# Summing squares over embeddings: on VectorE inside a tile, or by accumulating DMAs

## The chip, the cores and the metric

The kernel runs on one core of one Trainium2 chip. A core has TensorE (PE, matrix products), VectorE (DVE), ScalarE (ACT), GpSimd (POOL) and SyncE (SP), which run side by side, each through its own instructions in order, and wait for one another at semaphores. Sixteen DMA engines move data between DRAM, the on-chip memory SBUF and themselves; a DMA is issued by SP, ACT or POOL, and whoever needs its result waits for its semaphore. PE writes its products into PSUM, which has eight banks of 128 x 512 fp32 numbers.

The metric is the device time of one execution in microseconds, lower is better.

## What is computed

The reference, cut to what matters (batch b = 1024, features f = 512, outputs m = 512, embeddings e = 64, all fp32):

```
out_lin = x @ lin_w.T + lin_b
xv = einsum('bf,efm->bem', x, weight)
zp = einsum('bf,efm->bem', square(x), square(weight))
y = out_lin + 0.5 * sum(square(xv) - zp, axis=1)
```

The large part is `xv`: 64 products of 1024 x 512 by 512 x 512, whose squares are summed over the 64 embeddings. The second sum needs no product per embedding: the squares of weight are summed over e first (`w2_sum`), and one product with the squares of x closes the kernel.

## The kernel before, in words

**Groups.** The 64 embeddings' weights are seen as one matrix of 512 rows and 64 x 512 columns. A group takes 2048 of its columns, and there are 16 groups. Within a group the product of x (1024 x 512) with the group's block (512 x 2048) is done by two nested levels of a seven-product scheme (Strassen's, in Winograd's form): the outer level cuts the weights into four quadrants `w11`, `w12`, `w21`, `w22`, each in two halves `.0` and `.1` of 128 x 1024 numbers (128 partitions, two rows of 512 columns), 512 KB each. A group is thus eight loads of 512 KB (`load`, L378).

**Outer level.** `outer_sum` (L384) forms on VectorE the combinations T1 = w12 - w11, T2 = w22 - T1, then overwrites w12 with w22 - w12 and w21 with w21 - T2. The seven outer products, in the order 1, 6, 2, 7, 4, 5, 3 (`ORDER`), are seven calls of `tree` (L416) with the right operands w11, T2, w21, w12, w21 (overwritten by then), T1, w22.

**Inner level.** `tree` forms four combinations `t1` to `t4` of 128 x 512 on POOL (L427), issues seven pairs of matmuls into PSUM (L438), and lets ACT copy banks out (L287) and VectorE and POOL add the products up in `oa`, `ob`, `c`, `p` (sums with both operands in SBUF may go to either engine, L274; those that read PSUM go to VectorE). The trees for i = 2, 3, 4 and 5 end four result tiles each, one per `pos`: that is 16 tiles of 128 x 1024 per group, all entries of `xv` for this block.

**Sum over embeddings.** On the host the weights are laid out so that a block of 512 columns holds 8 outputs with their 64 embeddings side by side. So the sum over embeddings is a sum over 64 neighbouring columns of a tile. `finish` (L402) squares a result tile on ACT in place and has VectorE reduce it (L296) from 128 x 1024 to 128 x 16 numbers in `acc`, which SP stores to DRAM once per group (`acc_dram`, 128 KB). `w_squares` (L394) does the same for the eight weight halves: ACT squares a half into one of two buffers `wsq` and VectorE reduces it into `w2_sum`.

**Order of the work.** The instructions of each engine are put in order by a planner in the kernel (`Plan`, L27): each operation has a cost per engine it may run on, what it reads and writes, and, for a DMA, a time `land` until its data is there. The sequence of the matmuls is fixed by keys. Latest start times are worked out backward from it, and a list scheduler then takes, on each engine, the most urgent ready operation. Operations with a choice between VectorE and POOL go where the planner finds room. The order so found is then emitted, and each engine follows it strictly.

**Start and end.** Before the first group, x, `lin_w` and the bias are loaded and the linear part is computed and parked in DRAM (`lin_dram`). After the last group, x is loaded again and squared, `acc_dram` and `lin_dram` are read back, half-adds `lin + 0.5 * acc` run on VectorE (L546), the closing products of the squares of x with `w2_sum` follow on PE (L565), and the results are stored.

Of the kernel before, what the change touches and what calls it, by code (L numbers as in the profile page):

```python
# [23 lines left out]
PE, DVE, ACT, POOL, SP = "PE", "DVE", "ACT", "POOL", "SP"  # L24


class Plan:  # L27

    HOP = 0.18
# [138 lines left out]
def kernel(  # L175
# [7 lines left out]
):  # L183

    nc = tc.nc
    NG, NQ, _, NCB, KH, N = weight.shape
    B = xT.shape[1]
    M = out.shape[1]
    NB = B // P
    NK = 2 * KH
    MG = M // NG
    MI = MG // 4  # L210
    E = N // MI
    H = B // 2
    Q = B // 4

# [1 line left out]
    dram = ctx.enter_context(  # L216
        tc.tile_pool(name="dram", bufs=1, space=bass.MemoryType.DRAM)
    )
# [6 lines left out]
    buf = {}  # L225

    def make(name, shape, pool=sb):
        buf[name] = pool.tile(shape, F32, tag=name, name=name)
        return name

    def ring(tag, n, shape, pool=sb):
        names = [make(f"{tag}_{i}", shape, pool) for i in range(n)]
        state = [0]

        def take():
            state[0] += 1
            return names[(state[0] - 1) % n]

        return take
# [13 lines left out]
    make("b1", [P, G, N], ps)  # L253
    make("b3", [P, G, N], ps)
    b2_ring = ring("b2", 2, [P, G, N], ps)
    acc_ring = ring("acc", 2, [P, NB, MG])
    w2_sum = sb.tile([P, NK, M], F32, tag="w2_sum", name="w2_sum")
    bias = sb.tile([P, M], F32, tag="bias", name="bias_sb")
    acc_dram = dram.tile([P, NB, M], F32, tag="accd", name="accd")
    lin_dram = dram.tile([P, NB, M], F32, tag="lind", name="lind")  # L260

    plan = Plan()
# [21 lines left out]
    def act(o, i, func, reads, writes, cost=1.04):  # L284
        def emit(_):
            if func is None:
                nc.scalar.copy(o, i)  # L287
            else:
                nc.scalar.activation(o, i, func)  # L289

        plan.add({ACT: cost}, emit, reads, writes)

    def reduce(o, i, reads, writes):
        plan.add(
            {DVE: 1.14},
            lambda _: nc.vector.tensor_reduce(  # L296
                o, i.rearrange("p a (m e) -> p a m e", e=E), axis=AX.X, op=ALU.add
            ),
            reads, writes,
        )  # L300

    def dma(o, i, reads, writes, cost=2.4, land=1.5, queue=nc.sync):
        plan.add({SP: cost}, lambda _: queue.dma_start(o, i), reads, writes, land=land)
# [14 lines left out]
    for k in range(NK):  # L318
        q, r = divmod(k, KH)
# [15 lines left out]
    for g, bank in enumerate(lin_banks):  # L335
        o = ("ob2", "ob3", "c_0", "c_1")[g]
# [23 lines left out]
    for i in ORDER:  # L360
        x = buf[f"X{i}"]
# [11 lines left out]
    QUAD = ("w11", "w12", "w21", "w22")  # L373

    def w(g, q):
        return q + "ab"[g % 2] if q == "w22" else q

    def load(g):  # L378
        for q in (0, 1, 3, 2):
            for c in range(NCB):  # L380
                n = f"{w(g, QUAD[q])}.{c}"
                dma(buf[n], weight[g, q][:, c], (), (n,))

    def outer_sum(g, which):  # L384
        o, a, b = {
            1: ("T1", "w12", "w11"),
            2: ("T2", w(g, "w22"), "T1"),
            3: ("w12", w(g, "w22"), "w12"),
            4: ("w21", "w21", "T2"),
        }[which]  # L390
        for c in range(NCB):
            whole(f"{o}.{c}", f"{a}.{c}", f"{b}.{c}", True, DVE)

    def w_squares(g, q):  # L394
        row, col = divmod(QUAD.index(q), 2)
        for c in range(NCB):
            n, sq = f"{w(g, q)}.{c}", wsq_ring()
            act(buf[sq], buf[n], AF.Square, (n,), (sq,), 1.07)
            m = g * MG + (2 * col + c) * MI
            reduce(w2_sum[:, ts(row, KH), m:m + MI], buf[sq], (sq,), (("w2", row, m),))  # L400

    def finish(g, i, n, pos):  # L402

        row, col = {2: (0, 0), 3: (0, 1), 4: (1, 0), 5: (1, 1)}[i]
        q, cc = divmod(pos, 2)
        b, m = (row * 2 + q) * G, (col * 2 + cc) * MI
        act(buf[n], buf[n], AF.Square, (n,), (n,), 1.07)
        reduce(buf[acc_name[g]][:, b:b + G, m:m + MI], buf[n], (n,), ((acc_name[g], i, pos),))
# [4 lines left out]
    acc_name = {}  # L413
    acc_parts = [(i, pos) for i in (2, 3, 4, 5) for pos in range(4)]

    def tree(s, g, i):  # L416
        r = [f"{w(g, RHS[i])}.{c}" for c in range(NCB)]
# [33 lines left out]
        def outer_psum(b, pos):  # L451

            if i == 1:
                copy(f"oa{pos}", b)
            elif i == 5:
                for n in (f"oa{pos}", f"ob{pos}"):
                    whole(n, n, b, psum=True)
                finish(g, i, f"oa{pos}", pos)
            else:
                o = target(pos)  # L460
                whole(o, b, f"{ADDEND[i]}{pos}", psum=True)
                if i in (2, 4, 3):
                    finish(g, i, o, pos)

        def outer_sbuf(b, p, pos):

            if i == 1:
                whole(f"oa{pos}", b, p, psum=True)
            elif i == 5:
                whole(p, b, p, psum=True)  # L470
                for n in (f"oa{pos}", f"ob{pos}"):
                    whole(n, n, p)
                finish(g, i, f"oa{pos}", pos)
            else:
# [21 lines left out]
        outer_psum(b2, 2)  # L496

    for g in range(NG):
        acc_name[g] = acc_ring()
        load(g)  # L500
        outer_sum(g, 1)
        outer_sum(g, 2)
        w_squares(g, "w12")
        for idx, i in enumerate(ORDER):
            if i == 1:
                w_squares(g, "w11")
            if i == 2:
                w_squares(g, "w21")
            if i == 7:
                outer_sum(g, 3)  # L510
            if i == 4:
# [10 lines left out]
    last = acc_name[NG - 1]  # L522
    edge = M - MG
    acc_all = ("T2.0", "T2.1", w(NG, "w22") + ".0", w(NG, "w22") + ".1")
    lin_all = ("w21.0", "w21.1", "T1.0", "T1.1")
    for (h, q), n in xe.items():
        dma(buf[n], x_src[:, ts(q, KH), ts(h, H)], (), (n,))
    for g in range(NB // G):
        n, a = lin_all[g], acc_all[g]
        dma(buf[a][:, :, 0:edge], acc_dram[:, ts(g, G), 0:edge],  # L530
            tuple(("accd", x) for x in range(NG - 1)), (a,))
        dma(buf[n], lin_dram[:, ts(g, G), :], (), (n,))
# [9 lines left out]
    def add_acc(g, lo, hi, a, reads):  # L542
        l = buf[lin_all[g]][:, :, lo:hi]
# [8 lines left out]
    for g in range(NB // G):  # L552
        rows = {0: (2, 3), 1: (4, 5)}[g // 2]
        reads = tuple((last, i, 2 * (g % 2) + c) for i in rows for c in range(2))
        add_acc(g, edge, M, buf[last][:, ts(g, G), :], reads)

    out_dst = out.rearrange("(n p) m -> p n m", p=P)
    w2_parts = tuple(("w2", row, m * MI) for row in range(2) for m in range(M // MI))
    for g, bank in enumerate(("b3", "b1", "b2_0", "b2_1")):
        o = acc_all[g]  # L560
        h = g // 2
# [52 lines left out]
```

## Time and profile before

| | |
|---|---|
| device time, median of 2 runs | 1438.42 us (1438.36 to 1438.48) |
| profiled execution, span from first to last instruction | 1436.8 us (its own device time is not given beside the span) |
| PE busy | 1408.8 us, 98% |
| VectorE busy | 1245.7 us, 87% |
| POOL busy | 1149.6 us, 80% |
| ACT busy | 748.8 us, 52% |
| DMA, main queue (SP's): share of the 16 engines | 18.1% |
| moved in all | 83.54 MB |

How to read it. Busy time is the time in which an engine carried out instructions; issuing a DMA and waiting do not count. A group row of the profile gives source line, engine, operation, output <- inputs, shapes and count; then busy time in us and the mean of one in ns; then the idle time before these instructions and whom they waited for. A row of the waits reads "who waited <- for whom: us in total, times, longest". A row of a window gives its bounds, its length, the busy time of PE, PEld (the loading of weights into PE), DVE, ACT and POOL, PE's granted clock (1.00 is full), the share of the DMA engines and GB/s. A row of the chain of waits or of the order of time begins with start and duration in us. A row of the DMA issues ends with size and the time from issue to landing.

### The profile page before, as it was taken

The numbers are of one execution on the slowest core, as the hardware profiler recorded it, in microseconds if no ns is written. First come the engines' busy times: TensorE is split into PE (matmuls) and PEld (weight loads), VectorE is DVE, ScalarE is ACT, GpSimd is POOL, SyncE is SP. The second block draws the span as 40 slices with busy tenths as digits, with TensorE's granted clock in tenths as the row PEclk, the third lists the DMA queues.
The fourth block names the chain that finished last, engine by engine and source line by source line (L and its number), as shares of the span: only waits on it lengthen the run. The fifth ranks groups of instructions, "written<-read, shape, count | busy, mean of one in ns | idle before, by whom it ended". The sixth has DMA issues, their size and how long they took to land.

```text
span 1436.8 us, 10763 instructions
## 1 busy us (share of the span) xinstructions
PE 1408.8 (98%) x3264; PEld 619.3 (43%) x3264; DVE 1245.7 (87%) x1006; ACT 748.8 (52%) x756; POOL 1149.6 (80%) x691
## 2 busy tenths in 40 slices
PE   7999999999999999999999999999999999999998
PEld 3444444444444444444444444444444444444443
DVE  1899898998989899898988989899898888989984
ACT  1465554645545465564556555465554546556441
POOL 6988886878878688896878888687887868889781
PEclk9999999999999999999999999999999999999999
DMA  5311111111111112111111111111111111210221
GB/s 212 117 60 58 48 59 33 59 48 59 59 42 51 33 59 62 46 58 33 59 48 58 59 48 59 33 59 48 58 59 45 53 32 57 60 52 22 88 74 59
DMA packets 40377, 83.54 MB, mean 58 GB/s; under 512 B 18240, under 2 KB 19264, under 8 KB 40320
## 3 DMA queue, kind: packets, MB, share of 16 engines
q1 hardware_dynamic: 39664, 81.54, 18.1%
q10 hardware_dynamic: 576, 1.05, 0.2%
q8 instruction: 27, 0.44, 0.1%
q14 instruction: 30, 0.25, 0.1%
q0 software_dynamic: 80, 0.26, 0.0%
HBM read 76.68 MB, written 6.16 MB: 58 GB/s over the span
## 4 chain that ended last, share of the span: by engine, by line
PE 90%; POOL 4%; DVE 2%; issue 1%; ACT 1%; DMA 1%; DVEq 0%; POOLq 0%; SPq 0%
PE b L438 86%; POOL oa L274 3%; PE b L325 2%; PE b L565 2%; ACT p L287 1%; POOL t L274 1%; DMA ob<-lin_wT 0%; DVE p L274 0%; DMA T1.1_83<-lind 0%; DVE ob L274 0%; DVE w11.1_73 L536 0%; DVE w21.0_76 L274 0%; DVE oa L274 0%; DVE acc L296 0%; DVE w11.0_72 L536 0%
## 5 line engine op out<-in xcount | busy, mean ns | idle before, releaser
L438 PE MATMUL b<-t,X 128*128 128x512 f32 x1792 | 806.2, 592 | 2.0 <-DVE p L274 1.6
L438 PEld LDWEIGHTS b<-t,X 128*128 128x128 f32 x1792 | 340.0, 190 | 431.9 <-issue 415.0
L287 ACT COPY p<-b 128x1024 f32<-128x1024 f32 x224 | 225.6, 1007 | 266.1 <-PE b L438 226.8
L289 ACT ACTIVATE oa<-oa 128x1024 f32<-128x1024 f32 x128 | 131.9, 1054 | 165.3 <-DVE oa L274 90.9
L296 DVE TENSOR_REDUCE w_sum<-wsq 128x16 f32<-128x1024 f32 x128 | 154.8, 1211 | 29.0 <-ACT wsq L289 28.9
L287 ACT COPY b<-b 128x1024 f32<-128x1024 f32 x112 | 111.8, 998 | 91.1 <-PE b L438 85.2
L274 DVE TENSOR_TENSOR p<-b,p 128x1024 f32<-128x1024 f32 x96 | 117.0, 1218 | 43.4 <-PE b L438 43.4
L296 DVE TENSOR_REDUCE acc<-oa 128x16 f32<-128x1024 f32 x128 | 152.0, 1207 | 0.0
L438 PE MATMUL b<-w21.0_76,X 128*128 128x512 f32 x256 | 120.3, 592 | 0.0
L274 POOL TENSOR_TENSOR oa<-oa,p 128x1024 f32<-128x1024 f32 x32 | 102.8, 3212 | 1.8
L289 ACT ACTIVATE c<-c 128x1024 f32<-128x1024 f32 x64 | 67.7, 1058 | 67.8 <-DVE c L274 67.8
L274 POOL TENSOR_TENSOR oa<-p,oa 128x1024 f32<-128x1024 f32 x32 | 75.7, 2365 | 27.2 <-DVE p L274 26.9
L274 DVE TENSOR_TENSOR oa<-b,p 128x1024 f32<-128x1024 f32 x64 | 78.0, 1219 | 11.7 <-PE b L438 10.8
L274 POOL TENSOR_TENSOR c<-c,oa 128x1024 f32<-128x1024 f32 x32 | 75.4, 2357 | 13.8 <-DVE c L274 11.7
L274 POOL TENSOR_TENSOR oa<-oa,ob 128x1024 f32<-128x1024 f32 x32 | 76.4, 2387 | 6.9 <-DVE oa L274 6.9
L274 POOL TENSOR_TENSOR ob<-ob,oa 128x1024 f32<-128x1024 f32 x32 | 76.3, 2384 | 5.5 <-DVE ob L274 5.5
L274 POOL TENSOR_TENSOR t<-w21.0_76,t 128x512 f32<-128x512 f32 x32 | 40.8, 1275 | 48.3 <-PE b L438 48.3
L274 POOL TENSOR_TENSOR ob<-p,ob 128x1024 f32<-128x1024 f32 x32 | 75.7, 2364 | 0.5 <-DVE p L274 0.5
L296 DVE TENSOR_REDUCE acc<-ob 128x16 f32<-128x1024 f32 x64 | 75.9, 1209 | 0.0
L296 DVE TENSOR_REDUCE acc<-c 128x16 f32<-128x1024 f32 x64 | 74.8, 1208 | 1.1 <-ACT c L289 1.1
L438 PEld LDWEIGHTS b<-w21.0_76,X 128*128 128x128 f32 x256 | 48.6, 190 | 61.2 <-issue 61.2
L274 DVE TENSOR_TENSOR ob<-b,oa 128x1024 f32<-128x1024 f32 x32 | 39.1, 1223 | 40.5 <-PE b L438 39.8
(127 smaller groups left out, 2295.9 us busy)
## 6 DMA issues: line engine op xcount, KB each, us to landing
w11.0_72<-weight SPq DMA_DIRECT2D x16, 512.0 KB, 3.7
w11.1_73<-weight SPq DMA_DIRECT2D x16, 512.0 KB, 3.8
w12.0_74<-weight SPq DMA_DIRECT2D x16, 512.0 KB, 3.8
w12.1_75<-weight SPq DMA_DIRECT2D x16, 512.0 KB, 3.8
w21.0_76<-weight SPq DMA_DIRECT2D x16, 512.0 KB, 3.8
w21.1_77<-weight SPq DMA_DIRECT2D x16, 512.0 KB, 4.7
w22a.0_78<-weight SPq DMA_DIRECT2D x8, 512.0 KB, 3.8
w22a.1_79<-weight SPq DMA_DIRECT2D x8, 512.0 KB, 3.8
```

Source lines behind the costliest of these rows:

```text
L274: f(o, a, b)
L287: nc.scalar.copy(o, i)
L289: nc.scalar.activation(o, i, func)
L296: lambda _: nc.vector.tensor_reduce(o, i.rearrange("p a (m e) -> p a m e", e=E), axis=AX.X, op=ALU.add),
L325: nc.tensor.matmul(buf[bank][:, j, :], buf[f"oa{2 * h + q}"][:, r, ts((g * G + j) % (NB // 2), P)], buf[f"ob{q}"][:, r, :], start=(k == 0) ...
L438: nc.tensor.matmul(buf[b][:, j, :], buf[f"X{i}"][:, SLOT[p], ts(j, P)], op, start=first, stop=True, skip_group_check=True,)
L565: nc.tensor.matmul(buf[bank][:, j, :], buf[xe[h, k // KH]][:, k % KH, ts((g * G + j) % (NB // 2), P)], w2_sum[:, k, :], start=(k == 0), st ...
```

## The change

The host lays the weights out so that a block of 512 columns is one embedding with all its 512 outputs; a group is four embeddings, one pair of quadrant and half each. The sum over embeddings then is a sum of whole tiles. It is no longer done on VectorE: each squared tile is added to a running sum by a DMA that POOL issues with `accum_op=ALU.add` (the first tile of each sum by a plain copy from SP's queue). The squares of weight are added into `w2_sum` in SBUF, in two places (one per row of quadrants). The squares of the results are added into two DRAM sums `acc_dram[0]` and `acc_dram[1]`, in four places each. DMAs into the same place are put one after another by a dependence on the place (`key`). The eight last result tiles (trees 5 and 3 of the last group) are not stored but added on VectorE at the end (`tail`), and at the end both DRAM sums are read back whole.

```diff
-    MG = M // NG
-    MI = MG // 4
-    E = N // MI
...
-    acc_ring = ring("acc", 2, [P, NB, MG])
...
-    acc_dram = dram.tile([P, NB, M], F32, tag="accd", name="accd")
+    NS = 2
+    acc_dram = [
+        dram.tile([P, NB, M], F32, tag=f"accd{s}", name=f"accd{s}") for s in range(NS)
+    ]
...
-    def reduce(o, i, reads, writes):
-        plan.add(
-            {DVE: 1.14},
-            lambda _: nc.vector.tensor_reduce(
-                o, i.rearrange("p a (m e) -> p a m e", e=E), axis=AX.X, op=ALU.add
-            ),
-            reads, writes,
-        )
+    started = set()
+
+    def accumulate(o, i, reads, key):
+
+        if key in started:
+            plan.add(
+                {POOL: 0.9},
+                lambda _: nc.gpsimd.dma_start(o, i, accum_op=ALU.add),
+                reads, (key,), land=5.0,
+            )
+        else:
+            started.add(key)
+            dma(o, i, reads, (key,))
...
     def w_squares(g, q):
-        row, col = divmod(QUAD.index(q), 2)
+        row = QUAD.index(q) // 2
         for c in range(NCB):
             n, sq = f"{w(g, q)}.{c}", wsq_ring()
             act(buf[sq], buf[n], AF.Square, (n,), (sq,), 1.07)
-            m = g * MG + (2 * col + c) * MI
-            reduce(w2_sum[:, ts(row, KH), m:m + MI], buf[sq], (sq,), (("w2", row, m),))
+            accumulate(w2_sum[:, ts(row, KH), :], buf[sq], (sq,), ("w2", row))
+
+    tail = []
 
     def finish(g, i, n, pos):
 
-        row, col = {2: (0, 0), 3: (0, 1), 4: (1, 0), 5: (1, 1)}[i]
+        row = {2: 0, 3: 0, 4: 1, 5: 1}[i]
         q, cc = divmod(pos, 2)
-        b, m = (row * 2 + q) * G, (col * 2 + cc) * MI
+        pair = row * 2 + q
         act(buf[n], buf[n], AF.Square, (n,), (n,), 1.07)
-        reduce(buf[acc_name[g]][:, b:b + G, m:m + MI], buf[n], (n,), ((acc_name[g], i, pos),))
+        if g == NG - 1 and i in (5, 3):
+            tail.append((pair, n))
+        else:
+            accumulate(acc_dram[cc % NS][:, ts(pair, G), :], buf[n], (n,), ("acc", pair, cc % NS))
...
-        if g + 1 < NG:
-            names = tuple((acc_name[g], *k) for k in acc_parts)
-            dma(acc_dram[:, :, ts(g, MG)], buf[acc_name[g]], names, names + (("accd", g),))
...
+    def add_half(g, n):
+        l = buf[lin_all[g]]
         plan.add(
-            {DVE: 0.15 + 1.09 * (hi - lo) / N},
-            lambda _: nc.vector.scalar_tensor_tensor(l, a, 0.5, l, ALU.mult, ALU.add),
-            reads + (lin_all[g],), (lin_all[g],),
+            {DVE: 1.24},
+            lambda _: nc.vector.scalar_tensor_tensor(l, buf[n], 0.5, l, ALU.mult, ALU.add),
+            (n, lin_all[g]), (lin_all[g],),
         )
 
     for g in range(NB // G):
-        add_acc(g, 0, edge, buf[acc_all[g]][:, :, 0:edge], (acc_all[g],))
...
+        for s in range(NS):
+            dma(buf[acc_all[g]], acc_dram[s][:, ts(g, G), :], (("acc", g, s),), (acc_all[g],))
+            add_half(g, acc_all[g])
+    for pair, n in tail:
+        add_half(pair, n)
...
-    w = w.reshape(n_e, p, 2, n_k // 2, groups, 2, 2, m_in).transpose(4, 2, 5, 1, 6, 3, 7, 0)
+    w = w.reshape(groups, 2, 2, p, 2, n_k // 2, width).transpose(0, 4, 1, 3, 2, 5, 6)
```

Counted over the whole program: 384 reductions (256 of results, 128 of weights) and 15 stores of `acc` go; 366 accumulating DMAs of 512 KB on POOL (240 into the DRAM sums, 126 into `w2_sum`), 10 plain copies of 512 KB on SP, and 8 more half-adds of 128 x 1024 come. The planner also gives 27 of the sums of 128 x 1024 that POOL had to VectorE. PE's matmuls, ACT's copies and squares and the weight loads stay the same in number and size.

More of the change, by code (lines that the diff above doesn't have):

```diff
@@ L412 @@
     RHS = {1: "w11", 2: "w21", 3: "w22", 4: "w21", 5: "T1", 6: "T2", 7: "w12"}
-    acc_name = {}
-    acc_parts = [(i, pos) for i in (2, 3, 4, 5) for pos in range(4)]
     def tree(s, g, i):
@@ L515 @@
             tree(7 * g + idx, g, i)
-        if g + 1 < NG:
-            names = tuple((acc_name[g], *k) for k in acc_parts)
-            dma(acc_dram[:, :, ts(g, MG)], buf[acc_name[g]], names, names + (("accd", g),))
     xe = {(h, q): (f"w11.{q}", f"w12.{q}")[h] for h in range(2) for q in range(2)}
-    last = acc_name[NG - 1]
-    edge = M - MG
     acc_all = ("T2.0", "T2.1", w(NG, "w22") + ".0", w(NG, "w22") + ".1")
@@ L528 @@
     for g in range(NB // G):
[L529 to L532, printed above, removed]
+        dma(buf[lin_all[g]], lin_dram[:, ts(g, G), :], (), (lin_all[g],))
     for n in xe.values():
@@ L540 @@
         )
-    def add_acc(g, lo, hi, a, reads):
-        l = buf[lin_all[g]][:, :, lo:hi]
+    def add_half(g, n):
+        l = buf[lin_all[g]]
         plan.add(
-            {DVE: 0.15 + 1.09 * (hi - lo) / N},
-            lambda _: nc.vector.scalar_tensor_tensor(l, a, 0.5, l, ALU.mult, ALU.add),
-            reads + (lin_all[g],), (lin_all[g],),
+            {DVE: 1.24},
+            lambda _: nc.vector.scalar_tensor_tensor(l, buf[n], 0.5, l, ALU.mult, ALU.add),
+            (n, lin_all[g]), (lin_all[g],),
         )
     for g in range(NB // G):
-        add_acc(g, 0, edge, buf[acc_all[g]][:, :, 0:edge], (acc_all[g],))
[L552 to L555, printed above, removed]
+        for s in range(NS):
[3 more added lines that the diff above has]
+        add_half(pair, n)
     out_dst = out.rearrange("(n p) m -> p n m", p=P)
-    w2_parts = tuple(("w2", row, m * MI) for row in range(2) for m in range(M // MI))
+    w2_parts = (("w2", 0), ("w2", 1))
     for g, bank in enumerate(("b3", "b1", "b2_0", "b2_1")):
@@ L591 @@
     n_e, n_f, n_m = w.shape
-    p, n_k, width = 128, n_f // 128, 512
-    m_in = width // n_e
-    groups = n_m // (4 * m_in)
-    w = w.reshape(n_e, p, 2, n_k // 2, groups, 2, 2, m_in).transpose(4, 2, 5, 1, 6, 3, 7, 0)
+    p, n_k, width = 128, n_f // 128, n_m
+    groups = n_e // 4
+    w = w.reshape(groups, 2, 2, p, 2, n_k // 2, width).transpose(0, 4, 1, 3, 2, 5, 6)
     arrays = {
```

1 line of the change is left out of this document (removed).

## The prediction

> **What bounds the kernel now.** I read the busy shares first, then the chain that ended last, then one steady stretch of it, and last the waits.
>
> ```profile
> span 1436.8 us, 10763 instructions
> PE 1408.8 (98%) x3264; PEld 619.3 (43%) x3264; DVE 1245.7 (87%) x1006; ACT 748.8 (52%) x756; POOL 1149.6 (80%) x691
> PE 90%; POOL 4%; DVE 2%; issue 1%; ACT 1%; DMA 1%; DVEq 0%; POOLq 0%; SPq 0%
> ...
> 293.37 79.25 PE b L438 x184
> 373.24 3.29 POOL oa L274
> 377.52 1.00 ACT p L287
> 378.57 79.25 PE b L438 x184
> ...
> 300.00:385.20 85.20, 84.39 (x198) 37.15 (x197) 76.26 (x62) 46.46 (x48) 69.43 (x42) 1.00 0.17 51
> ```
>
> The reader is to see a kernel that is TensorE from end to end. The chain repeats every 85.20 us (293.37 to 378.57), which is one of the 16 groups; in such a stretch PE is busy 84.39 us at a granted clock of 1.00, DVE 76.26, POOL 69.43. So DVE, whose reductions the change takes away, is not the bound. Nor can much be won: 2% less than the median of 1438.42 is 1409.7, and PE alone is busy 1408.8. The question is therefore whether PE keeps being fed. The sums are made against the profiled execution (span 1436.8); the median lies 1.6 above that span, which I take as what lies around it, so an amount that is added to the span is added to 1438.
>
> **What is removed.**
>
> ```profile
> L296 DVE TENSOR_REDUCE w_sum<-wsq 128x16 f32<-128x1024 f32 x128 | 154.8, 1211 | 29.0 <-ACT wsq L289 28.9
> L296 DVE TENSOR_REDUCE acc<-oa 128x16 f32<-128x1024 f32 x128 | 152.0, 1207 | 0.0
> L296 DVE TENSOR_REDUCE acc<-ob 128x16 f32<-128x1024 f32 x64 | 75.9, 1209 | 0.0
> L296 DVE TENSOR_REDUCE acc<-c 128x16 f32<-128x1024 f32 x64 | 74.8, 1208 | 1.1 <-ACT c L289 1.1
> accd<-acc SPq DMA_DIRECT2D x15, 128.0 KB, 2.4
> ```
>
> 384 reductions, 457.5 us of DVE, and 15 stores of 128 KB. DVE gets 27 sums of 128x1024 from POOL and 8 more half-adds at the end; at 1.2 to 2.3 us each (rows below) that is some 40 to 80 us, and DVE falls to about 850 of 1437. On the end of the kernel this gain is worth nothing, because PE did not wait for a reduction:
>
> ```profile
> PEld b L438 <- POOL t L274: 9.6, 31, 1.2
> PEld b L438 <- DVE w_sum L296: 1.2, 5, 0.2
> ACT wsq L289 <- DVE w_sum L296: 1.8, 4, 1.2
> ```
>
> The third row is the one to remember: a square buffer came free after a 1.2 us reduction, and ACT waited for one 1.8 us in the whole run.
>
> **What is added.** 384 squares of 128x1024 (512 KB each) are summed elsewhere: 8 by half-adds on DVE, 10 first ones by plain copies on SP's queue, and 366 (126 into w2_sum, 240 into the two DRAM sums) by accumulating DMAs issued by POOL. Per group that is 23. Each has three prices: POOL's time to issue, the DMA engines' time, and the time until it lands.
>
> ```profile
> 305.79 0.33 SPq L303 DMA_DIRECT2D w11.0_72<-weight  x1
> ...
> L308 POOL DMA_DIRECT2D bias_sb<-lin_b x1 | 0.7, 677 | 0.8 <-POOLq L603 0.8
> L274 POOL TENSOR_TENSOR ob<-ob,p 128x1024 f32<-128x1024 f32 x17 | 41.1, 2417 | 2.3 <-DVE p L274 2.3
> L274 DVE TENSOR_TENSOR oa<-b,p 128x1024 f32<-128x1024 f32 x64 | 78.0, 1219 | 11.7 <-PE b L438 10.8
> L274 DVE TENSOR_TENSOR ob<-ob,p 128x1024 f32<-128x1024 f32 x15 | 34.2, 2282 | 0.0
> L274 POOL TENSOR_TENSOR t<-w12.0_74,t 128x512 f32<-128x512 f32 x16 | 20.4, 1273 | 4.5 <-PE b L438 4.5
> POOL t L274 <- PE b L438: 118.8, 124, 3.2
> POOL t L274 <- DVE w12.0_74 L274: 47.0, 15, 3.1
> POOL oa L274 <- DVE p L274: 26.9, 15, 1.8
> POOL t L274 <- DVE w21.0_76 L274: 18.6, 16, 1.2
> ```
>
> *POOL's issue.* The only DMA that POOL issues before took it 677 ns. 366 x 0.677 = 247.8 us. Bounds: 0.33 us, what SP needs to issue a load in the order of time, and 1.27 us, a POOL sum of half size. I take 0.677, the only row of POOL's own. POOL gives up 27 x 2.42 = 65 us of sums. So POOL goes from 1149.6 to 1332, that is 83.3 us of work per group of 85.2, where it had 69.43. Before, POOL waited 118.8 + 47.0 + 26.9 + 18.6 = 211.3 us, 13.2 per group, for PE and for DVE's sums. These waits are dependences and do not vanish; DVE answers sooner now, so I keep half, 6.6. POOL's own account is then 89.9 us per group, 4.7 more than PE's 85.2.
>
> *DMA engines and landing.*
>
> ```profile
> 14.00:18.00 4.00, 4.00 (x11) 1.75 (x10) 0.28 (x1) 0.00 (x0) 4.00 (x5) 1.00 1.04 414
> q1 hardware_dynamic: 39664, 81.54, 18.1%
> w11.0_72<-weight SPq DMA_DIRECT2D x16, 512.0 KB, 3.7
> bias_sb<-lin_b POOLq DMA_DIRECT2D x1, 256.0 KB, 7.4
> ```
>
> With the DMA engines full (share 1.04) plain transfers ran at 414 GB/s, so 524,288 bytes take 1.27 us of all sixteen. An accumulation must also read what it adds to. No row shows one. Bounds: 1.27 us if that read costs nothing, 3.8 if source read, target read and write follow one another. I take 2.53: two reads for one write, on engines that a plain copy already fills with one of each.
> [...]
> Per group the DMA engines then have 23 x 2.53 + 8 loads x 1.27 = 68 us of work, 0.71 of the 96 us that a group comes to below; before it was under 0.2. Landing: a plain 512 KB load lands 3.7 us after its issue with the engines nearly idle; the second read makes it 5.0. To that comes the transfer that is in service when it arrives, 0.71 x 1.27 = 0.9, and about one accumulation ahead of it in POOL's queue, 2.5 (in the changed order of POOL's instructions many follow one another: three in a row, or two, between sums). Together 8.4 us; the bias row's 7.4, in the busy start, is the nearest one that POOL issued. The planner's code books 0.9 + 5.0.
>
> *The serial chain.* Accumulations into one place must wait for each other. The eight squares of weight per group share two places, and two square buffers. In the changed order POOL's eight weight accumulations stand so: after the one of w11's second half come 23 other POOL instructions (14 half sums, 5 whole sums, 4 accumulations), then w21, w21, w22, w22, each with a wait for the one before, then w12 (another place, no such wait), w12, w11, w11, each again with a wait. That is six serial steps and one stretch of other work. POOL works in order, so behind each waiting accumulation stand half sums t that PE needs next. One step is issue 0.68 + landing 8.4 = 9.1 us; six are 54.6. The stretch is 14 x 1.27 + 5 x 2.4 + 4 x 0.68 = 32.5 us of POOL, and with the share of waiting that POOL has in a group today (15.8 of 85.2, 19%) 38.7. Three of the squares wait for their buffer, so that ACT's square lies in the chain: 3 x 1.06 = 3.2.
>
> ```profile
> 420.98 1.06 ACT L289 ACTIVATE wsq<-w12.1_75 128x1024 f32<-128x1024 f32 x1
> ...
> 443.03 1.05 ACT L289 ACTIVATE wsq<-w21.0_76 128x1024 f32<-128x1024 f32 x1
> ...
> 416.07 2.03 DVE L274 TENSOR_TENSOR w21.0_76<-w21.0_76,T2.0_84 128x1024 f32<-128x1024 f32 x1
> ```
>
> Before, the squares from w12 to w21 took 22 us (420.98 to 443.03), long before w21 is overwritten (416.07 and again 85.2 later); after, they are what that overwriting, and through it POOL's t for tree 4 and PE, waits for. The chain's round is 54.6 + 38.7 + 3.2 = 96.5 us. It and POOL's account run beside each other, so the larger sets the group: 96.5 - 85.2 = 11.3 us, times 16 = 181. **1438 + 181 = 1619, say 1620 us.**
>
> **What costs nothing.** The host's other layout leaves loads of the same size and number (8 of 512 KB per group). ACT squares as often; but it too works in order, and its copies out of PSUM stand behind squares that wait for a buffer. That is inside the chain's 11.3. DVE's writes into oa, ob and c now wait for an accumulation instead of a reduction; with 8.4 us against a reuse of a tree or more later, I price them at nothing, up to 3 us per group if landing exceeds 10 us. SP's weight loads stand behind the ten first copies in the first group only. At the end 8 loads of 512 KB instead of 4 of 480 columns, and 16 half-adds of 1.2 us; they lie beside the last trees and the closing products:
>
> ```profile
> 1404.63 27.48 PE b L565 x64
> ```
>
> Price zero, up to 10 us if the last sums land late.
>
> **The rivals.**
>
> *First: accumulations are as cheap as copies* (1.27). Landing is then about 3.7 + 0.5 + 1.3 = 5.5, six steps 37, the round 79, shorter than 85.2; POOL's account sets, 4.7 x 16 = 75: 1512 us, 1470 to 1540 with half or all of POOL's old waits. For it: the code's 5.0; against: the second read.
>
> *Second, the other side: not slower.* POOL's 83.3 us of work fit into 85.2 if it keeps less than 1.9 of its 13.2 us of waiting, DVE with 400 us to spare answering at once, and the chain takes under 85.2, which by the sum above means a landing under 6.5 us. Then 1438, at best some 1430 by the 0.8 us per group in which PE is idle. It decides at these two points. Against it: 118.8 of the 211.3 us are waits for PE, which DVE cannot shorten.
>
> *Third: the transfers set the pace.* At 3.8 us the DMA engines have 23 x 3.8 + 10 = 97 us per group, and landing is 3.7 + 2.5 + 1.3 + 3.8 = 11.3; six steps 72, the round 114: 1438 + 16 x 29 = 1900. At 3.1 us it is about 1750.
>
> **How the numbers follow.** Forecast, 1540 to 1700: 0.50. First rival 0.21. Second 0.07, of which 0.01 is a time under 1410. Third, above 1700: 0.22. The range 1475 to 1770 leaves out the second rival and about half of the third, 0.18. A difference under 2% (1410 to 1467) is about what a measurement of this kernel cannot tell from none: faster 0.01, same 0.06, slower 0.93.
>
> **What the changed profile would show.** PE's share near 87%, with idle of several us ahead of products with w21, b and t in each group, and a round near 96 us in the chain of waits. POOL's accumulating DMAs near 0.7 us each; POOL near 1330 us. The DMA share near 0.7 to 0.8 and some 8 us to landing. ACT waiting for DMAs ahead of wsq, POOL for DMAs ahead of its own. DVE near 850. The forecast is wrong if POOL's issues take 1.27 us (POOL 97 us per group before any wait), if landing is under 6.5 us, or if PE's granted clock falls in the new gaps, which no row of before shows.

## The result and the profile after

The changed kernel takes **1735.49 us** (1733.64 to 1737.33) against 1438.42 us: 1.206 times as long, with an interval of 1.203 to 1.210. The profiled execution is the one of 1737.33 us; its span is 1735.1 us, 298.3 more than before.

The page of the changed kernel: span and busy shares, the queue of POOL's DMAs and that of SP's, and the chain that ended last, by engine and then by line:

```profile
span 1735.1 us, 11093 instructions
PE 1489.4 (86%) x3264; PEld 634.0 (37%) x3264; DVE 1054.6 (61%) x657; ACT 748.8 (43%) x756; POOL 1374.8 (79%) x1030
q0 software_dynamic: 52784, 192.18, 61.3%
q1 hardware_dynamic: 25568, 87.04, 15.4%
PE 30%; DMA 29%; POOL 17%; DVE 10%; issue 10%; ACT 3%; POOLq 0%; SPq 0%; DVEq 0%; ACTq 0%
PE b L421 29%; DMA w_sum<-wsq 14%; DMA accd<-oa 9%; POOL t L250 6%; DMA accd<-c 4%; POOL ob L250 2%; DVE w21.0_76 L250 2%; POOL accd L276 2%; DVE ob L250 2%; POOL oa L250 2%; PE b L538 2%; POOL w_sum L276 2%; POOL c L250 1%; DVE p L250 1%; DVE oa L250 1%
```

No engine is full any more: PE fell from 98% to 86%, POOL stands at 79%, the DMA engines at 61.3 + 15.4 = 76.7%. The chain, which was 90% PE, is now a relay of PE, DMA, POOL and DVE. The time went to two places. PE's idle time rose from 1436.8 - 1408.8 = 28.0 us to 1735.1 - 1489.4 = 245.7, that is +217.7. And PE's busy time rose by 80.6 us with the same matmuls: they ran at a lower granted clock, a mean of 0.950 where it was 1.000. The groups of instructions show that, first of before, then of after (busy us, mean ns | idle ahead and its releasers):

```profile
L438 PE MATMUL b<-t,X 128*128 128x512 f32 x1792 | 806.2, 592 | 2.0 <-DVE p L274 1.6 <-POOL t L274 0.4
L274 DVE TENSOR_TENSOR w21.0_76<-w21.0_76,T2.0_84 128x1024 f32<-128x1024 f32 x16 | 33.3, 2080 | 0.0
```

```profile
L421 PE MATMUL b<-t,X 128*128 128x512 f32 x1792 | 864.9, 624 | 177.7 <-POOL t L250 75.6 <-DVE oa L250 46.6 <-ACT b L263 26.7
L276 POOL DMA_DIRECT2D accd<-oa x120 | 136.8, 1253 | 18.9 <-ACT oa L265 18.8
L276 POOL DMA_DIRECT2D w_sum<-wsq x126 | 124.0, 1013 | 146.7 <-DMA w_sum<-wsq 116.5 <-PE b L421 13.3 <-issue 5.9
L276 POOL DMA_DIRECT2D accd<-c x60 | 83.1, 1386 | 1.9 <-ACT c L265 1.9
L276 POOL DMA_DIRECT2D accd<-ob x60 | 64.3, 1261 | 56.4 <-ACT ob L265 54.9 <-issue 1.5
L250 DVE TENSOR_TENSOR w21.0_76<-w21.0_76,T2.0_84 128x1024 f32<-128x1024 f32 x16 | 85.7, 5358 | 0.0
```

The matmuls with t went from 592 to 624 ns, and PE stood 177.7 us ahead of them, where it had stood 2.0. The spans of POOL's issues are 1.01 to 1.39 us on average, the four groups together 136.8 + 124.0 + 83.1 + 64.3 = 408.2 us. That is not POOL's time for issuing, for a span can overlap the next instruction's: in the order of time one issue begins at 799.32 and lasts 0.85 us, and the span of the sum behind it begins at 799.91. The first experiment gives POOL's own time. The last row is a DVE sum that took 2.08 us on average before and takes 5.36 now; I come back to it.

The DMA issues of the changed kernel (the last number is the median time from issue to landing):

```profile
w_sum<-wsq POOLq DMA_DIRECT2D x126, 512.0 KB, 8.0
accd<-oa POOLq DMA_DIRECT2D x120, 512.0 KB, 9.4
accd<-ob POOLq DMA_DIRECT2D x60, 512.0 KB, 10.4
accd<-c POOLq DMA_DIRECT2D x60, 512.0 KB, 7.8
w11.1_73<-weight SPq DMA_DIRECT2D x16, 512.0 KB, 9.7
```

The accumulations land after 8 to 10 us, and the plain loads of weights, on a queue of their own, are late as well: up to 9.7 us, for w11.1, which landed after 3.8 us before.

The waits of the changed kernel (who waited <- for whom: us in total, times, longest):

```profile
POOL w_sum L276 <- DMA w_sum<-wsq: 116.5, 36, 7.1
ACT wsq L265 <- DMA w_sum<-wsq: 105.9, 48, 7.4
ACT oa L263 <- DMA accd<-oa: 98.8, 15, 7.5
DVE ob L250 <- DMA accd<-ob: 96.1, 30, 10.1
PEld b L421 <- POOL t L250: 95.1, 37, 8.8
DVE oa L250 <- DMA accd<-oa: 31.2, 15, 4.9
```

The first two are the weights' sum: POOL behind the accumulation before, ACT for its square buffer. The third, fourth and last are buffers of *results*, oa and ob, that may not be overwritten until their accumulation has landed. They come to 226.1 us, as much as the weights' 222.4.

Some pieces of the chain of waits (start, us, what):

```profile
791.07 5.82 DVE w21.0_76 L250
...
866.29 9.10 DMA w_sum<-wsq
...
875.95 10.74 DMA w_sum<-wsq
...
927.15 8.12 DMA accd<-c
...
951.49 11.77 DMA accd<-oa
...
974.64 15.59 DMA accd<-oa
...
997.99 6.99 DVE w21.0_76 L250
...
1414.69 6.62 DVE w21.0_76 L250
```

Two groups lie between the first and the second row of w21.0, and six between the first and the last: (1414.69 - 791.07) / 6 = 103.9 us each, 18.7 above the 85.2 of before; 16 x 18.7 = 299 is the whole loss. In the two groups shown the chain goes, among others, through two landings into w_sum and three into a DRAM sum. Over the whole span it passes 25 landings into w_sum (249.0 us) and 21 into the DRAM sums (246.8 us).

Windows of the changed kernel (bounds, length, busy time of PE, PEld, DVE, ACT, POOL; then the granted clock, the share of the DMA engines, GB/s):

```profile
784.00:791.00 7.00, 6.48 (x11) 2.79 (x12) 3.43 (x3) 3.27 (x4) 5.50 (x5) 0.76 0.77 149
...
950.00:975.00 25.00, 19.06 (x38) 8.04 (x37) 17.64 (x9) 11.47 (x13) 18.14 (x18) 0.86 0.94 180
```

The granted clock is 0.76 in the first window, which begins in a gap of PE of 2.26 us (782.26 to 784.52), and 0.86 in the second, in which PE stands for 25.00 - 19.06 = 5.94 us. So a wait is paid twice here: over the execution PE is idle 217.7 us longer and busy 80.6 us longer. Closer up, behind PE's gap of 4.38 us before 799.42 the granted clock is 0.51 up to 802.84 and 1.00 from there to 806.00; behind the one of 2.26 us it is 0.95 up to 785.86 and 0.52 from there to 789.27.

### The profile page after: what moved, and what is told of

It is laid out like the page before. It is cut to its first block, busy times and chain, and to the rows that moved or that the text cites. A ratio compares the mean times of both kernels' runs of the same rounds, so it can differ in the third digit from the quotient of the medians.

```text
span 1735.1 us, 11093 instructions
## 1 busy us (share of the span) xinstructions
PE 1489.4 (86%) x3264; PEld 634.0 (37%) x3264; DVE 1054.6 (61%) x657; ACT 748.8 (43%) x756; POOL 1374.8 (79%) x1030
## 3 DMA queue, kind: packets, MB, share of 16 engines
q0 software_dynamic: 52784, 192.18, 61.3%
q1 hardware_dynamic: 25568, 87.04, 15.4%
## 4 chain that ended last, share of the span: by engine, by line
PE 30%; DMA 29%; POOL 17%; DVE 10%; issue 10%; ACT 3%; POOLq 0%; SPq 0%; DVEq 0%; ACTq 0%
PE b L421 29%; DMA w_sum<-wsq 14%; DMA accd<-oa 9%; POOL t L250 6%; DMA accd<-c 4%; POOL ob L250 2%; DVE w21.0_76 L250 2%; POOL accd L276 2%; DVE ob L250 2%; POOL oa L250 2%; PE b L538 2%; POOL w_sum L276 2%; POOL c L250 1%; DVE p L250 1%; DVE oa L250 1%
## 5 line engine op out<-in xcount | busy, mean ns | idle before, releaser
L421 PE MATMUL b<-t,X 128*128 128x512 f32 x1792 | 864.9, 624 | 177.7 <-POOL t L250 75.6
L421 PEld LDWEIGHTS b<-t,X 128*128 128x128 f32 x1792 | 351.4, 200 | 656.6 <-issue 543.5
L276 POOL DMA_DIRECT2D w_sum<-wsq x126 | 124.0, 1013 | 146.7 <-DMA w_sum<-wsq 116.5
L276 POOL DMA_DIRECT2D accd<-oa x120 | 136.8, 1253 | 18.9 <-ACT oa L265 18.8
L276 POOL DMA_DIRECT2D accd<-ob x60 | 64.3, 1261 | 56.4 <-ACT ob L265 54.9
L250 DVE TENSOR_TENSOR ob<-b,p 128x1024 f32<-128x1024 f32 x32 | 39.2, 1225 | 99.6 <-PE b L421 62.5
L265 ACT ACTIVATE ob<-ob 128x1024 f32<-128x1024 f32 x64 | 67.4, 1058 | 68.1 <-DVE ob L250 67.7
L250 DVE TENSOR_TENSOR w21.0_76<-w21.0_76,T2.0_84 128x1024 f32<-128x1024 f32 x16 | 85.7, 5358 | 0.0
L276 POOL DMA_DIRECT2D accd<-c x60 | 83.1, 1386 | 1.9 <-ACT c L265 1.9
L250 DVE TENSOR_TENSOR oa<-b,ob 128x1024 f32<-128x1024 f32 x32 | 39.2, 1224 | 74.1 <-PE b L421 53.4
```

The costliest lines, as they stand in the source:

```text
L250: f(o, a, b)
L276: lambda _: nc.gpsimd.dma_start(o, i, accum_op=ALU.add),
L421: nc.tensor.matmul(buf[b][:, j, :], buf[f"X{i}"][:, SLOT[p], ts(j, P)], op, start=first, stop=True, skip_group_check=True,)
```

## The experiments

The theory of the prediction was that the weights' accumulations wait for each other in two places, which stretches the group. The rivals, with the result in hand: **POOL** has too much to do (issues on top of its sums); **the DMA engines** are too slow when they add; **the order of the work** is wrong, because the planner books an accumulation at 0.9 us of POOL and 5.0 us to landing, so that everything that needs a buffer again is placed too early; and the accumulations disturb others **by being there**, whoever waits for them. An experiment's time is that of one execution; the two of the changed kernel lie 3.7 us apart, and I read nothing into differences of a few us. The kernel before, on the same chips, took 1438.06 to 1438.42 us.

### Copies in place of accumulations

```diff
-                lambda _: nc.gpsimd.dma_start(o, i, accum_op=ALU.add),
+                lambda _: nc.gpsimd.dma_start(o, i),
```

> The changed kernel with one thing different: POOL's 366 accumulating DMAs copy instead of adding (the sums over embeddings are left out, only the last tile of each place stays). Order, waits, places and bytes written are the same; the second read of each DMA goes. Theory L (the round is set by waiting for accumulations to land, and landing is long because each keeps the DMA engines busy 2.9 us): the DMA price falls to about 1.3 us, landing from 8 to 10 us to 5 or 6, and the time from 1735 to 1500 to 1580. Theory P (POOL's own time sets it: 408 us of issuing): POOL issues the same number, so 1680 or more.

Measured: 1569.49 us. The busy shares, the queue of POOL's DMAs and their largest group:

```profile
PE 1455.3 (93%) x3264; PEld 629.4 (40%) x3264; DVE 980.5 (63%) x657; ACT 747.3 (48%) x756; POOL 1267.9 (81%) x1030
q0 software_dynamic: 52784, 192.18, 31.0%
L276 POOL DMA_DIRECT2D w_sum<-wsq x126 | 70.1, 557 | 55.5 <-DMA w_sum<-wsq 19.3 <-ACT b L263 18.3 <-PE b L421 11.2
```

This settles two prices. A copy of 512 KB costs 0.310 x 1567.3 / 366 = 1.33 us of all sixteen engines, an accumulation 0.613 x 1735.1 / 366 = 2.91, 2.19 times as much. The prediction's factor of 2, two reads for one write, was its author's estimate: no run shows the second read, for the page counts the same 192.18 MB in POOL's queue with copies and with accumulations. What is measured is the 2.19. And POOL issues a copy in 0.55 us (202.8 us in 366). The order is that of the changed kernel, where POOL is busy 1374.8 - 1267.9 = 106.9 us longer, 0.29 us per DMA. So an accumulation takes POOL about 0.55 + 0.29 = 0.85 us; this is an estimate, which puts all of the difference down to the issues. The add is worth 1735 - 1569 = 166 us, POOL's part and the DMA engines' together. But 131 of the 297 us remain when nothing is added, in an order in which waits for DMAs are short (19.3 where there were 116.5). So the accumulation's price is not all of it.

### Accumulations that nobody waits for, in the kernel before

The kernel before, with an accumulation of `X1` (loaded long before) into a scratch tile of DRAM behind 356 of POOL's half sums t; in the second form each moves 32 KB, not 512. The result and its order are those of before.

```diff
+    def idle_add():
...
+            nc.gpsimd.dma_start(scratch[:, k % 12], spare, accum_op=ALU.add)
...
+                emit(e)
+                idle_add()
```

```diff
-            nc.gpsimd.dma_start(scratch[:, k % 12], spare, accum_op=ALU.add)
+            nc.gpsimd.dma_start(scratch[:, k % 12, 0, 0:64], spare[:, 0, 0:64], accum_op=ALU.add)
```

> The kernel before, with its reductions, plus 356 accumulating DMAs of 512 KB on POOL, one behind each of 23 of the 28 half sums t per group, from a tile that never changes into 12 scratch places that nobody reads; the order on PE, ACT and DVE is that of before, and each such DMA waits only for the one 8 issues earlier. Price of the DMAs' presence alone. Theory P: POOL goes from 69 to about 95 us of work per group of 85.2, so 1600 or more. Theory L: nobody waits for a landing, so at most 1480. A time between would be the price of POOL's issues and of slower weight loads together, without any wait for the sums.

> As e2_idle (the kernel before with 356 accumulating DMAs that nobody waits for), but each moves only 128 x 64 numbers (32 KB) instead of 512 KB: POOL issues as many, the DMA engines have almost nothing to do. If the 226 us of e2_idle come from POOL's time for issuing: 1620 or more. If they come from the DMA engines' load (weight loads that landed in 5 to 10 us instead of 3.7, and POOL held up in issuing by full queues, 1.57 us each): at most 1500.

Measured: 1664.08 us with 512 KB, 1590.88 us with 32 KB. The group of the issues, the landing of one weight load and a stretched DVE sum, with 512 KB:

```profile
L383 POOL DMA_DIRECT2D scr<-X x356 | 524.8, 1567 | 0.0
w21.1_77<-weight SPq DMA_DIRECT2D x16, 512.0 KB, 9.9
L274 DVE TENSOR_TENSOR w12.1_75<-w22b.1_81,w12.1_75 128x1024 f32<-128x1024 f32 x8 | 70.9, 8862 | 0.0
```

and with 32 KB:

```profile
PE 1459.0 (92%) x3264; PEld 627.9 (40%) x3264; DVE 1360.5 (86%) x1006; ACT 744.8 (47%) x756; POOL 1459.3 (92%) x1047
L383 POOL DMA_DIRECT2D scr<-X x356 | 583.6, 1746 | 0.0
w21.1_77<-weight SPq DMA_DIRECT2D x16, 512.0 KB, 4.7
```

Presence alone costs a great deal. With hardly any bytes, and weights that land as before (4.7 us), the time rises by 153 us, somewhat less than the 1620 or more that was expected of POOL's price alone. POOL is 92% busy, 1459.3 - 1149.6 = 309.7 us more than before, 0.87 us for each of the 356 issues (with 512 KB 0.83, from a busy time of 1444.7); DVE is busy 115 us longer with the same work. That is POOL's price, not the DMA engines'. The bytes add 73 us; the weights then land after 9.9 us. The changed kernel should pay less for the same: there POOL has fewer sums, and the planner has booked some of the issues' time, here none. How much less these runs don't show.

### All sums that may go to either engine on DVE

```diff
-        plan.add({e: c for e, c in costs.items() if only in (None, e)}, emit, (a, b), (o,),
+        plan.add({DVE: costs[DVE]}, emit, (a, b), (o,),
```

> The changed kernel, but all sums of 128x1024 that could go to either engine go to DVE, so POOL has only the half sums t and the DMAs (its work falls by about 500 us, DVE gains about 230). Theory P: 1500 to 1580. Theory S (DVE's sums of two SBUF tiles are held up for as long as POOL's sums follow one another: w21 5.36 us, w12 5.6 to 7.1 us where they took 2.1 and 1.2): part of the gain, 1620 to 1680, with these means back near 2 us. Theory L: landing stays at 8 to 10 us and the time above 1680.

Measured: 1742.94 us. The page:

```profile
PE 1495.7 (86%) x3264; PEld 644.5 (37%) x3264; DVE 1208.2 (69%) x839; ACT 746.9 (43%) x756; POOL 917.1 (53%) x848
```

POOL has lost 182 sums and 458 us of work, and nothing is gained. So in the order that the planner makes of this, POOL's total work is not the bound. (It moved instead into waiting: POOL's wait for the accumulation into w_sum before, 116.5 us in the changed kernel, is 186.6 us here.)

### The weights' squares alone

```diff
         if key in started:
+            if key[0] == "acc":
+                return
```

> The changed kernel without the 240 accumulations of result squares (that sum is left out; the first tile of each place is still copied); the 126 of the weights, their two places and two buffers stay, planned as in the changed kernel with 0.9 and 5.0. The prediction's chain alone: six serial landings per group. With the DMA engines less busy a landing should be near 5.5 us, so the chain of six is 37 us and hidden: 1440 to 1480 if the chain matters only through long landings. If the chain of the weights is what sets the round by itself: 1600 or more. If it is the results' buffers (oa, ob, c) and POOL's issues that cost: at most 1480 here.

Measured: 1466.43 us. The issues:

```profile
w_sum<-wsq POOLq DMA_DIRECT2D x126, 512.0 KB, 4.5
L278 POOL DMA_DIRECT2D w_sum<-wsq x126 | 112.4, 895 | 45.0 <-DMA w_sum<-wsq 39.9 <-ACT wsq L265 4.0 <-issue 0.9
```

The two places and two buffers of the chain that the prediction put the loss on are all here, in an order that the planner makes anew, and the loss is 28 us. The chain that ended last passes no landing into w_sum, where it passed 25. For without the 240 results an accumulation lands after 4.5 us, and the issue takes 0.90: about what the planner books. By the prediction's sum a landing under 6.5 us makes the chain shorter than PE's 85.2; a group here takes 85.2 + 28 / 16 = 87. With 240 fewer DMAs on the engines and on POOL the chain hardly hurts. This agrees with the prediction's sum and does not refute it: what the chain costs with landings of 8 us, this run cannot tell.

### Twice as many places

```diff
-    NS = 2
+    NS = 4
...
-            accumulate(w2_sum[:, ts(row, KH), :], buf[sq], (sq,), ("w2", row))
+            o = w2_sum[:, ts(row, KH), :] if c == 0 else w2_dram[:, ts(row, KH), :]
+            accumulate(o, buf[sq], (sq,), ("w2", row, c))
...
+            s = cc + 2 * (i in (2, 4))
```

> The changed kernel with twice the places: the weights' sums in four places (two in SBUF, two in DRAM, added up at the end), the results' in sixteen. As many DMAs, buffers as before, planned with 0.9 and 5.0. Theory L1 (what costs is one accumulation waiting for the one before it in the same place, six in a row per group): 1580 to 1640. Theory L2 (what costs is that a buffer, wsq, oa, ob or c, comes free only when its accumulation has landed): within 3% of 1735.

Measured: 1715.35 us. The waits for DMAs:

```profile
DVE oa L252 <- DMA accd<-oa: 148.3, 33, 10.1
DVE ob L252 <- DMA accd<-ob: 104.5, 18, 15.4
ACT wsq L267 <- DMA w2d<-wsq: 77.5, 38, 5.9
```

(At the end the DRAM half of the weights' sum is read back and added.) With half as many accumulations in a row into one place, 20 us are gained. What waits most now is not the next accumulation into the place but the next writer of the buffer: DVE for oa and ob, ACT for wsq. So accumulations that follow each other in one place were not the main thing. But the weights' squares still share two buffers, and the chain that ended last passes 32 of their landings here (327 us), more than the 25 of the changed kernel. That the buffers hold the time up fits these waits; no run has more buffers, so it isn't shown.

### What the planner is told

The same operations, booked otherwise: landing alone (8.5 in place of 5.0), both prices as the profile's spans show them (1.15 and 8.5), and both still larger (1.35 and 11.0).

```diff
-                {POOL: 0.9},
+                {POOL: 1.15},
                 lambda _: nc.gpsimd.dma_start(o, i, accum_op=ALU.add),
-                reads, (key,), land=5.0,
+                reads, (key,), land=8.5,
```

> As e4_prices, but only the landing is told as it measured (8.5); POOL's price stays at 0.9. If the too short landing in the plan is what cost the 162 us between the changed kernel and e4_prices: 1560 to 1610. If it was POOL's too low price: 1680 or more.

> The changed kernel, only the planner is told what an accumulation measured: 1.15 us on POOL and 8.5 us until it lands, instead of 0.9 and 5.0. Same operations, another order. If the order made for 5.9 us is what makes the waits cost so much, 1600 to 1660; if the resource is short whatever the order (L or P), within 2% of 1735.

> The changed kernel, its planner told 1.35 us for POOL's issue and 11.0 us for landing, beyond what e4_prices was told (1.15 and 8.5) and near the largest values that its profile still shows. All operations are those of the changed kernel. Theory A (what the order lost is won back by e4_prices; the rest is what the DMAs cost by being there): within 15 us of e4_prices' 1573. Theory B (the rest, too, is an order that books its DMAs too short): a good part of the remaining 135 us goes, 1520 or less. Above 1600: a longer booking holds the buffers for too long in the plan, and 8.5 was near the best.

Measured: 1644.56 us with the landing alone, **1573.21 us with both prices**, 1634.90 us with the largest. The page, one of the landings and one of the waits with both prices:

```profile
span 1571.4 us, 11077 instructions
PE 1449.4 (92%) x3264; PEld 624.5 (40%) x3264; DVE 977.9 (62%) x703; ACT 743.9 (47%) x756; POOL 1279.6 (81%) x984
...
accd<-oa POOLq DMA_DIRECT2D x120, 512.0 KB, 9.4
...
POOL w_sum L276 <- DMA w_sum<-wsq: 40.5, 15, 3.7
```

162 of the 297 us go when the planner books other prices, more than was expected; the landing alone gives 91, between the two ranges expected of it. The DMAs are no faster: accd<-oa lands after 9.4 us as before. Only the order is different (46 sums are on DVE instead of POOL; moving sums alone gained nothing above). PE's busy time falls by 40 us with the gaps, its idle time by 123.7. Of the waits, POOL's for the accumulation before falls from 116.5 to 40.5 us; the three for oa and ob hardly change, from 226.1 to 210.7. Raising the prices further loses 62 us again, though hardly a wait for an accumulation is left there (50.8 us for ob, 1.5 for oa). So the waits added up do not measure the loss, a longer booking is no free margin, and the 135 us that are left do not go with a longer booking.

What the 162 us show is that the order matters that much. That the true prices give the better order isn't shown: 1.15 us is the mean span of an issue, above the 0.85 of POOL's time worked out above, which the planner's 0.9 already met, and yet it gains 71 us over 0.9. Every pair of prices gives another order of everything, and only these were tried; how much is the right price and how much a fortunate order stays open.

### With the prices 1.15 and 8.5: sums on DVE, more places, the weights on DVE

Three of the edits above, each on top of the prices 1.15 and 8.5. In the last the squares of weight are added on DVE:

```diff
-            accumulate(w2_sum[:, ts(row, KH), :], buf[sq], (sq,), ("w2", row))
+            plan.add(
+                {DVE: 1.14},
+                lambda _, o=o, sq=sq: nc.vector.tensor_add(o, o, buf[sq]),
+                (sq, ("w2", row)), (("w2", row),), both=True,
+            )
```

> As e4_prices, with all optional sums of 128x1024 on DVE (some 137 fewer on POOL, which then has only its half sums and the issues). Theory A in its form 'POOL's own time is the rest': POOL loses about 137 x 2.4 = 330 us of work, and the time falls to 1480 to 1520. Theory D (not POOL's sums but its issues, which hold back DVE's sums with two inputs in SBUF, and the late loads): 1560 to 1600, as DVE takes over sums that are stretched.

> As e4_prices, with twice the places for both sums (weights: two in SBUF, two in DRAM; results: sixteen), so that two accumulations into one place follow each other half as often. [...] Theory B (the serial chain is what is left once the order is right): 1500 to 1530.

> As e4_prices (prices 1.15 and 8.5), but the squares of weight are added by DVE into w2_sum (128 sums of 128x1024, about 1.2 to 2.3 us each) and only the 240 results by accumulating DMAs. The result is complete. Theory A (the rest of the loss goes with the number of DMAs that POOL issues and the engines carry): 240 of 366 remain, so 1438 + 135 x 240 / 366 = 1527. Theory B (what is left comes from the two places of the weights, where accumulations still wait for each other): near 1450 to 1480. Theory C (the results' buffers oa, ob, c carry the rest): 1555 to 1575, no gain.

Measured: 1599.74 us with the sums on DVE, 1576.08 us with the places, 1603.96 us with the weights on DVE, against 1573.21 with the prices alone. First the page of the sums on DVE, then a group of the weights on DVE:

```profile
PE 1468.3 (92%) x3264; PEld 637.7 (40%) x3264; DVE 1114.9 (70%) x838; ACT 742.8 (46%) x756; POOL 933.0 (58%) x849
```

```profile
L387 DVE TENSOR_TENSOR w_sum<-w_sum,wsq 128x1024 f32<-128x1024 f32 x126 | 308.8, 2458 | 34.2 <-ACT wsq L265 32.8
```

The kernel with POOL at 58% is no faster, and neither is the one with more places: of the 135 us that are left neither POOL's sums nor accumulations in a row into one place are the cause by themselves. The third run missed all that was expected of it: with 126 DMAs fewer it is 31 us slower. It doesn't count as evidence against the DMAs' presence, for it brings an error of its own: DVE's added sums are booked at 1.14 us and take 2.46, so the order rests on a wrong number again; that this is what costs the 31 us isn't shown. How the 135 us divide (POOL's issues, stretched sums, late weights, the clock at 0.98) stays open. No version with the whole result came near the kernel before.

## Why the prediction was right, and where it was not

Forecast 1620, range 1475 to 1770, slower 0.93; measured 1735.49. Direction and range held; the likeliest value was 115 us low, and the result lies outside the forecast's own case (1540 to 1700), at a time that was given to the third rival. That the number came as near as it did is in part luck: terms that were left out stand where a part of the chain was missing.

- **What bounds, and what the removed reductions are worth:** right. DVE lost its reductions and nothing was gained, since PE was the bound. But DVE fell to 1054.6 us, not to about 850: its remaining sums became longer.
- **POOL's issue:** mis-sized. 0.677 us came from a plain DMA; accumulations took POOL about 0.85 us, some 310 us against 247.8, and POOL's busy time is 1374.8 against 1332. The sign that was named, 1.27 us per issue and 97 us of POOL per group, did not come: in the two groups of the window 791 to 998 POOL is busy 167.41 us, 83.7 per group. The sum has a slip here: 83.3 is a sixteenth of all of POOL's work, with start and end, while the 69.43 beside it is a window in the middle. From that window the sum is 69.43 + (247.8 - 65) / 16 = 80.9, POOL's account is 87.5 and not 89.9, and the first rival's 1512 becomes some 1475. That POOL's own account does not set the group was right as far as one order shows it: without 182 of its sums the time is 1743.
- **The DMA engines' price:** 2.91 us, predicted 2.53, between the bounds 1.27 and 3.8. No run shows the two reads that the 2.53 was worked out from. The share is 76.7%, predicted 0.71.
- **Landing:** 8.0 us for the weights, predicted 8.4. The planner's 5.0 was seen as the wrong number, but what follows from it was not drawn: not only the chain, every reuse of a buffer in the order rests on it. Booking 8.5 gains 91 us, and 1.15 with it 162.
- **The serial chain of the weights, +181:** this is the step that held only in part as a mechanism, though its number is near. The round is 103.9 us against 96.5, and the waits that were named are there (116.5 and 105.9 us). But the prediction has six landings of each group in a row, 96 in all, and the chain that ended last passes 25 (249.0 us), about one and a half per group; almost as much time goes through landings into the DRAM sums (246.8 us). With half as many accumulations in a row into a place only 20 us are gained. What the chain costs by itself with landings of 8 us stays open, for its two buffers were never more. (A slip in the sum: with POOL waiting 15.8 of 85.2 us, 32.5 us of work take 32.5 x 85.2 / 69.4 = 39.9 us and not 38.7, which would make it some 20 us more.)
- **"DVE's writes into oa, ob and c ... I price them at nothing":** wrong. The waits for accd<-oa and accd<-ob are 226.1 us, 14.1 per group, against a bound of "up to 3 us per group", and the chain of waits passes through landings of 8.12, 11.77 and 15.59 us there. But the waits are not the price: with both prices in the planner 210.7 us of them remain, and the time is 162 us lower. What they cost by themselves no run shows.
- **The clock:** named as what would make the forecast wrong, and not priced. It is 80.6 of the 298.3 us.
- **The first rival** (as cheap as copies: 1512): with real copies the same order takes 1569, above that rival's 1540. So even there the sum was short. POOL's issue was not the reason, 0.55 us against 0.677. PE was busy 46.5 us longer than before and idle 112.0 us where it was 28.0; what made it wait there stays open.
- **The third rival** (transfers set the pace): the time fell in its range, but its mechanism didn't happen; the engines are 76.7% busy, and a better order of the same transfers takes 1573.

## What to carry to other kernels

Moving work to DMAs that add is not free even when an engine is relieved: here each 512 KB cost POOL about 0.85 us, the DMA engines 2.9 us, and held its source for 8 to 10 us, against one 1.2 us reduction on an engine that had time. Where a planner orders the work by booked times, the bookings alone can move the time by more than half of the loss (162 of 297 us here), and not always for the better when they grow: measure the price, and try the order made with it. A span of the profile is not yet a price where spans overlap: compare the engine's busy time with and without the operation. And price a wait for a buffer by its landing time under load, for every buffer that the DMA reads, not only for the place it writes.

## What was not expected of the hardware

**DVE sums stretched by POOL.** The order of time in the changed kernel, first DVE, then POOL (start, us, instruction):

```profile
791.07 5.82 DVE L250 TENSOR_TENSOR w21.0_76<-w21.0_76,T2.0_84 128x1024 f32<-128x1024 f32 x1
796.80 1.21 DVE L250 TENSOR_TENSOR w21.1_77<-w21.1_77,T2.1_85 128x1024 f32<-128x1024 f32 x1
...
790.87 2.62 POOL L250 TENSOR_TENSOR oa<-p,oa 128x1024 f32<-128x1024 f32 x1
793.18 2.61 POOL L250 TENSOR_TENSOR ob<-ob,oa 128x1024 f32<-128x1024 f32 x1
```

The same kind of sum takes 1.21 us in the second row and 5.82 in the first, which ends at 796.89, 1.1 us after POOL's second sum (795.79). It looks as if the whole DVE sum ran after POOL had finished two sums in a row. The run with all sums that may go to either engine on DVE bears it out: there w21.0 takes 1.22 us on average (19.4 us in 16). Sums with an operand in PSUM are not stretched in the changed kernel (1.21 to 1.23 us on average in every group of 128 x 1024); of those with both operands in SBUF some are, 5.36 us on average for this sum, and some are not (oa<-p,oa 1.23 us in 15). In the kernel with accumulations of 512 KB that nobody waits for, w12.1 takes 8.86 us; there the order of the sums is that of before, where the longest mean of a group with both operands in SBUF was 3.36 us (T2.0, 3364 ns). That POOL's sums hold DVE's up fits these numbers; how they would do so no run shows.

**Accumulations are dearer to issue than copies:** about 0.85 us of POOL against 0.55, and no less for 32 KB (0.87) than for 512 KB (0.83 in the same kernel). The spans of 1.57 and 1.75 us in those two runs cannot be POOL's time: 356 x 1.75 = 623 us on top of the 1149.6 of before would be more than the whole span of 1589.1, and 356 x 1.57 = 559 more than that of 1662.3. Why the issue is dearer isn't settled.

**The clock fell with the gaps:** a mean of 0.950 over the execution, where it was 1.000, though PE was still 86% busy; PE was idle for 245.7 us, where it had been for 28.0.
